# A higher planned cost for indirect DMAs in the list scheduler of a fused MoE, attention, MoE kernel

## The chip, the cores and the metric

The kernel runs on one core of a Trainium2 chip. A core has five engines with an instruction queue each: PE (TensorE, matmuls), DVE (VectorE), ACT (ScalarE), POOL (GpSimd) and SP (SyncE, which here only issues DMAs). Each engine takes its own queue in order, and the engines wait for each other by semaphores. The metric is the device time of one execution in microseconds (us). The kernel before was run nine times: median 531.88 us, lowest 528.12, highest 533.92.

## The reference

4,096 tokens (8 blocks of 512) with 128 features pass three layers, in f32:

```
x = x + 0.5 * ffn(layernorm(x))        # first expert layer,  key 0 in the kernel
x = x +  attention(layernorm(x))
x = x + 0.5 * ffn(layernorm(x))        # second expert layer, key 1

ffn(x):  n = layernorm(x) * gamma + beta
         probs = softmax(n @ router_w.T)            # 8 experts
         top_v, top_i = top_k(probs, 2);  gates = softmax(top_v)
         out = sum over e of comb[:, e] * ((silu(n @ g_e) * (n @ u_e)) @ down_e)    # d_ff 384
               + shared swiglu(n)                                                   # d_ff 128
attention(x): windows of 128 tokens; q, k, v; scores; the 32 largest scores of a row kept;
         softmax; times v; leaky relu; + x; layernorm
```

## The kernel before

**Stages.** The 8 blocks form two groups of 4 blocks (2,048 tokens); in names, `key` is the expert layer (0, 1) and `g` the group. For each (key, g) the kernel does this:

- `norm` normalizes a block, writes the rows to DRAM (`rows`), turns them on PE (`nTp`) and computes the logits (`lg`).
- `route` works out on DVE, with a few small matmuls (`rank`, `inv`), which token stands in which slot when the tokens are sorted by expert. It leaves `src` (the token of each slot) and `dst` (where a result goes).
- `experts` and `pair` do the expert work: 32 slot tiles of 128, and 39 pairs of a tile and an expert. A tile is fetched by an indirect DMA that POOL issues (`fetch`, L846: `xg<-rows,src`), four to a chunk. The chunk is turned on PE (`xTp`) and copied by ACT (`xT`). A pair is three matmuls for the gate (`pg`), three for the up projection (`pu`), a silu on ACT, a product on DVE (`s`), and three matmuls down (`y`), all 128x128x128 in f32. Four pairs share a `y` bank; ACT copies it (`yb`), and POOL issues one indirect DMA for each pair, which scatters the rows to DRAM (`put`, L962: `ys<-yb,dst`). Between two puts stands a 0.09 us memset.
- `shared` is the shared expert of a block (`pgs`, `pus`, `ysh`). `fetch_back` loads the scattered results (`yg`, SP or ACT queue), which waits for all 39 puts of the group; `combine` adds them on DVE (blocks 4 and 6 of the second layer on PE instead, `sum`, L1030).
- Between the two layers every block goes through `attention`, whose largest part is DVE's: four rounds of the 8 largest and their removal (`am8`, `tk`), each over four windows.

There are 128 fetches and 156 puts, 284 indirect DMAs in all.

**The order of the work.** No loop gives the order. Each step is recorded with `plan.op(engine, us, ...)`, where `us` is a planned duration, together with what it reads and writes, and gets a due time: the latest due time of what it needs plus a delay, or a floor set by the caller. `Plan.schedule` then plays the recorded steps: at each turn it takes the engine that can start earliest and, of the steps that can start there, the one due first. Every engine's queue is written out in the order found. The planned durations therefore decide the order, and nothing in the chip's run corrects it.

**The fillers.** `Plan.emit` does one more thing with the planned times. Where PE's planned idle time before a step is more than `IDLE` = 0.75 us, it puts matmuls into PE's queue that nobody reads (`unread`, L448), one for each `IDLE_US` = 0.22 us of the planned idle time less 0.4 us. They keep PE busy while it is planned to wait. They wait for nothing, and nobody waits for them but PE's queue. The profile counts two instructions for each.

```
idle = o.start - end
if idle > IDLE:
    us = IDLE_US * (COLD_FACTOR if o.start < COLD else 1.0)
    for _ in range(int((idle - IDLE_LEFT) / us)):
        self.idle()
```

**The constants.** `PACE` is the step of the due times from one fetch to the next for the four (key, g); `LAG`, `STRETCH` space the due times of the attention blocks; `ROUTE_STRETCH` and `ROUTE_B` those of the routing; `NORM_*` and `SHARED`, `SHARED1` those of the norms and the shared experts; `PAIRS`, `PUTS` parts of the routing; `FINISH` the last combination of the first group. A fetch is planned at 1.28 us of POOL (L846's `pool(1.28, ...)`), a put at 1.33 us.

Of the kernel before, what the change touches and what calls it, by code (L numbers as in the profile page):

```python
# [40 lines left out]
CH = 4  # L41
# [9 lines left out]
HANDOVER = {"PE": 0.25, "ACT": 0.2, "DVE": 0.2, "POOL": 0.25, "SP": 0.0}  # L51
OVERLAP = {"PE": 0.0, "ACT": 0.08, "DVE": 0.07, "POOL": 0.0, "SP": 0.0}
TABLE_LOAD = 1.28
COLD, COLD_FACTOR = 26.0, 1.8


# [2 lines left out]

PACE = (1.79, 2.74, 2.27, 0.89)
LAG, STRETCH, ROUTE_STRETCH = 9.73, -0.34, 3.22
NORM_B, NORM_LAG, NORM_STRETCH = 7.11, 1.83, 1.14
SHARED = ((28.42, 6.74), (33.75, 24.46))
SHARED1 = ((114.02, 8.44), (5.88, 23.46))
ROUTE_B = 38.08
PAIRS, PUTS = 0.5, 4.89
FINISH = 18.87


class Buf:
# [23 lines left out]
class Plan:  # L96
# [47 lines left out]
    def schedule(self):  # L144
# [38 lines left out]
        while len(order) < len(ops):  # L183
# [26 lines left out]
            if o.table and o.table != table:  # L210
                table = o.table
                o.start += TABLE_LOAD
            clock[o.eng] = o.start + us - OVERLAP[o.eng]
# [39 lines left out]
def kernel(  # L253
# [25 lines left out]
    plan = Plan(  # L279
        {  # L280
            "nT": 2 * GB,
            "h": GB, "a0": GB, "a1": GB, "a2": GB, "v": GB, "sc": GB,
            "ss": 2,
            **{t: 8 for t in ("st", "mv", "ve", "rstd", "nb", "am8", "nm", "rs")},
            "s": 4, "wt": WT, "xg": 4, "yb": 3, "yg": 4, "lanes": 4,
            **{t: 2 for t in ("lgs", "gates", "src", "off", "row", "to", "dst")},
            **{
# [12 lines left out]
    def pe(us, fn, r, w, **k):  # L300
        return plan.op("PE", us, fn, r, w, **k)

    def act(us, fn, r, w, **k):
        return plan.op("ACT", us, fn, r, w, **k)
# [4 lines left out]
    def pool(us, fn, r, w, **k):  # L309
        def run():  # L310
            last_put.clear()
            fn()

        return plan.op("POOL", us, run, r, w, **k)
# [4 lines left out]
    def buf(shape, tag, name, dtype=F32):  # L319
        return Buf(sb, shape, tag, name, dtype)  # L320

    def bank(kind, name):
        return Buf(ps, [P, W, P], "ps", name, kind=f"ps_{kind}")
# [208 lines left out]
    def norm(key, b, on_act=True):  # L532

        g, i = divmod(b, GB)
        r = routed[key, g]
        nm = f"_{key}_{b}"

        xb, xk = (lambda: xs[b]), [("x", b)]  # L540
        mv = stats(xb, xk, nm)
        rstd = scales(mv, nm, eps2)
        n = buf([P, W, H], "a0", f"n1_{key}_{b}")
        if on_act:
            normalize_act(n, xb, xk, rstd, shifts(mv, rstd, nm))
        else:
            normalize(n, xb, xk, mv, rstd)
        rows_t = r.rows[1 : 1 + GT, :].rearrange("(b p w) h -> b p w h", p=P, w=W)
        wr = load(0.6, lambda: rows_t[i], n, [n], [("rows", key, g, i)], lat=2.9)
        nT = r.nT[b] = buf([P, W, P], "nT", f"nT_{key}_{b}")  # L550
        tp = transposed(n, [n], f"nTp_{key}_{b}", hold=[nT])
        act(
            0.77,
            lambda: nc.scalar.activation(  # L554
                nT(), tp(), AF.Identity, bias=gb[:, 1:2], scale=gb[:, 0:1]
            ),
            [tp, "gb"], [nT],
        )
        lg = bank("m", f"lg_{key}_{b}")

        def logits():
            for w in range(W):
                nc.tensor.matmul(lg()[:, w, 0:NE], nT()[:, w, :], rwT, start=True, stop=True)  # L563

        pe(1.06, logits, [nT, "rwT"], [lg])
        dve(
            0.19,
            lambda: nc.vector.tensor_copy(r.lgs()[:, i * W : (i + 1) * W, :], lg()[:, :, 0:NE]),
            [lg], [(r.lgs, i)],
        )  # L570
        return wr

    def shared(key, b):

        nT = routed[key, b // GB].nT[b]
        pg, pu, ysh = (bank("m", f"{t}_{key}_{b}") for t in ("pgs", "pus", "ysh"))
        s, xk = buf([P, W, P], "ss", f"ss_{key}_{b}"), ("x", b)
        mm = nc.tensor.matmul
        up = pe(0.85, lambda: mm(pg(), gus[:, 0, :], nT(), start=True, stop=True),  # L579
                [nT, "gus"], [pg], hold=[s])  # L580
        act(0.6, lambda: nc.scalar.activation(s(), pg(), AF.Silu), [pg], [s], table="silu")
        pe(0.85, lambda: mm(pu(), gus[:, 1, :], nT(), start=True, stop=True),  # L582
           [nT, "gus"], [pu], after=[(up, 0.0)])
        dve(0.69, lambda: nc.vector.tensor_tensor(s(), pu(), s(), ALU.mult), [pu, s], [s])

        def down():
            for w in range(W):
                mm(ysh()[:, w, :], s()[:, w, :], dns, start=True, stop=True)  # L588

        pe(0.88, down, [s, "dns"], [ysh])  # L590
        dve(0.69, lambda: nc.vector.tensor_tensor(xs[b], ysh(), xs[b], ALU.add), [ysh, xk], [xk])
# [238 lines left out]
    before_ = [None] * 5  # L830

    def experts(key, g, pace):

        r, nm = routed[key, g], f"{key}_{g}"
        rows = [("rows", key, g, i) for i in range(-1, GB)]
        sizes = list(FIRST) if (key, g) == (0, 0) else []
        while sum(sizes) < NS:
            sizes.append(CH)
        fetched = []
        for c, n in enumerate(sizes):  # L840
            t0 = sum(sizes[:c])
            xg = buf([P, CH, H], "xg", f"xg_{nm}_{c}")
            for j in range(n):

                def fetch(t=t0 + j, j=j, xg=xg):
                    nc.gpsimd.indirect_dma_start(  # L846
                        xg()[:, j, :], None, r.rows,
                        bass.IndirectOffsetOnAxis(ap=r.src()[:, t : t + 1], axis=0),
                    )

                before_[2] = pool(1.28, fetch, [r.src, *rows], [(xg, j)], lat=3.6,
                                  after=[(before_[2], pace)])
                fetched.append(before_[2])
            tp = bank("m", f"xTp_{nm}_{c}")

            def turn(t0=t0, n=n, xg=xg, tp=tp):
                for w in range(n):
                    nc.tensor.transpose(tp()[:, w, :], xg()[:, w, :], ident)  # L858

            pe(0.11 * n, turn, [(xg, j) for j in range(n)], [tp])  # L860

            def fill(t0=t0, n=n, tp=tp):
                nc.scalar.activation(  # L863
                    xT[:, t0 * P : (t0 + n) * P].rearrange("p (w t) -> p w t", t=P),
                    tp()[:, 0:n, :], AF.Identity, bias=gb[:, 1:2], scale=gb[:, 0:1],
                )

            act(0.25 + 0.13 * n, fill, [tp, "gb"], [("xT", t0 + j) for j in range(n)])

            upto = NT if t0 + n == NS else t0 + n  # L870
            for t in range(t0, upto):
                first = t0 + (t - t0) // CH * CH
                pair(r, key, g, t, pace, fetched[min(t, NS - 1)], first, min(first + CH, upto))

    def pair(r, key, g, t, pace, came, first, upto):

        nm, group = f"{key}_{g}", f"ys_{key}_{g}"
        c, j = divmod(t, CH)
# [4 lines left out]
        y, yb = r.y, r.yb  # L883
# [73 lines left out]
        for i in range(a, b):  # L957
            def put(t=c * CH + i, i=i):
                if last_put:
                    nc.gpsimd.memset(apart, 0.0)  # L960
                last_put.append(t)
                ins = nc.gpsimd.indirect_dma_start(  # L962
                    r.ys, bass.IndirectOffsetOnAxis(ap=r.dst()[:, t : t + 1], axis=0),
                    yb()[:, i, :], None,
                ).ins

                tc.declare_no_dep(ins, group=group, reason="rows of other tokens")
                tc.add_to_no_dep_group(group, ins)

            plan.op("POOL", 1.33, put, [(yb, i), r.dst], [(group, c * CH + i)], lat=3.4)  # L970

    def fetch_back(key, b):

# [167 lines left out]
    def blocks(g):  # L1141
        return range(g * GB, (g + 1) * GB)
# [6 lines left out]
    rows = [norm(0, b, b % 2 == 1) for b in blocks(0)]  # L1149
    load_rest(rows)  # L1150
    def at(us, stretch=1.0):
        plan.floor, plan.stretch = us, stretch

    for g in range(NG):
# [4 lines left out]
        for i, b in enumerate(blocks(g)):  # L1159
            at(SHARED[g][0] + i * SHARED[g][1])  # L1160
            shared(0, b)
        at(ROUTE_B * g, 2.0 * g)
        route(0, g)
        at(0.0)
    for g in range(NG):
        experts(0, g, PACE[g])
    for g in range(NG):
# [14 lines left out]
        for i, b in enumerate(blocks(g)):  # L1182
            at(start + SHARED1[g][0] + SHARED1[g][1] * i)
            shared(1, b)
        at(0.0)
        experts(1, g, PACE[2 + g])
        diag = {b: weigh(b) for b in blocks(g) if b in LAST_ON_PE}
        for b in sorted(blocks(g), key=lambda b: b % 2):
            if g == 0:
                at(plan.ops[-1].due + FINISH, 2.0)  # L1190
            if b in diag:
# [42 lines left out]
```

## Time and profile before

| | |
|---|---|
| median of nine runs | 531.88 us |
| the profiled execution | 532.83 us, its span 531.0 us |
| PE busy | 501.5 us (94%), 31.8 us of it fillers |
| DVE, ACT, POOL busy | 376.5 us (71%), 276.0 us (52%), 369.2 us (70%) |
| granted PE clock | 0.992 of full speed |
| first expert pair starts | 49.30 us |
| first pair of (1,0) | 293.53 us |
| first pair of (1,1) | 426.47 us |
| last `y` ends, last `sum` begins | about 511.5 us, 520.4 us |

The span runs from the first to the last profiled instruction. A row of a group of instructions reads: line, engine, operation, what it writes <- what it reads, how often, then total busy time, mean nanoseconds of one, the engine's idle time just before them, and what ended most of that. A row of a timeline reads: start, duration, engine, line, operation, names, count, and in brackets the idle time of the engine before it and what ended it; rows of one engine may overlap a little, since an instruction can start before the one ahead has ended.

### The profile page before, as it was taken

How to read it: one execution, taken by the hardware profiler on the slowest of the kernel's cores; microseconds unless marked ns; L12 is line 12 of the kernel's file. 1: busy time of each engine (PE TensorE's matmuls, PEld its weight loads, DVE VectorE, ACT ScalarE, POOL GpSimd, SP SyncE). 2: the span in 40 equal slices, each digit the busy share in tenths (PEclk: the TensorE clock that was granted, in tenths of full speed). 3: DMA queues.
4: the chain of work that ended last, by engine and by line, in shares of the span. 5: the costliest groups of instructions: out<-in, count | busy, mean ns of one | idle time of the engine just before them, and what ended most of it. 6: DMA issues, size and time to landing. Idle time of an engine off the chain costs nothing.

```text
span 531.0 us, 13493 instructions
## 1 busy us (share of the span) xinstructions
PE 501.5 (94%) x4064; PEld 466.1 (88%) x4064; DVE 376.5 (71%) x1440; ACT 276.0 (52%) x588; POOL 369.2 (70%) x484
## 2 busy tenths in 40 slices
PE   3999999999979999899998999999999989999996
PEld 2878899999969899889987889989998889999996
DVE  6569944984418999995489799998478768445413
ACT  4822433333324799896630588897665224343310
POOL 7204787788876888878645788888845777878840
PEclk9999999999989999999999899999999999999999
DMA  7940211111359534537627545364775272211125
GB/s 231 329 159 22 56 50 46 51 49 51 95 158 339 185 106 136 187 105 226 206 66 233 156 124 153 102 204 137 215 221 153 76 232 84 74 51 51 52 86 188
DMA packets 39611, 72.27 MB, mean 136 GB/s; under 512 B 7604, under 2 KB 17848, under 8 KB 39544
## 3 DMA queue, kind: packets, MB, share of 16 engines
q1 hardware_dynamic: 29880, 51.73, 31.6%
q0 software_dynamic: 9088, 18.63, 11.5%
q10 hardware_dynamic: 576, 1.05, 0.5%
q8 instruction: 38, 0.62, 0.5%
q14 instruction: 29, 0.24, 0.2%
HBM read 54.86 MB, written 16.52 MB: 134 GB/s over the span
## 4 chain that ended last, share of the span: by engine, by line
PE 57%; DVE 23%; ACT 7%; POOL 4%; issue 4%; DMA 3%; DVEq 0%; POOLq 0%; ACTq 0%
PE pg L924 15%; PE y L940 14%; PE pu L924 14%; DVE tk L1088 5%; DVE am L1084 4%; DMA xg<-rows,src 3%; PE unread L448 3%; DVE s L935 2%; PE lg L563 2%; POOL ys L962 2%; PE pgs L579 2%; PE ysh L588 2%; POOL xg L846 2%; PE xTp L858 2%; PE pus L582 2%
## 5 line engine op out<-in xcount | busy, mean ns | idle before, releaser
L962 POOL DMA_INDIRECT ys<-yb,dst x156 | 160.4, 1028 | 60.1 <-ACT yb L954 29.4
L846 POOL DMA_INDIRECT xg<-rows,src x128 | 129.2, 1009 | 71.5 <-issue 31.8
L924 PE MATMUL pg<-xT,wt 128*128 (+1 forms) x936 | 134.3, 280 | 4.8 <-ACT xT L863 1.6
L924 PE MATMUL pu<-xT,wt 128*128 (+1 forms) x936 | 131.3, 277 | 0.0
L940 PE MATMUL y<-ew,s 128*128 x936 | 130.0, 276 | 1.0 <-DVE s L935 0.7
L924 PEld LDWEIGHTS pg<-xT,wt 128*128 128x128 f32 x936 | 119.0, 194 | 11.7 <-issue 4.3
L932 ACT ACTIVATE s<-pg 128x384 f32<-128x384 f32 x156 | 75.9, 491 | 99.9 <-PE pg L924 94.4
L940 PEld LDWEIGHTS y<-ew,s 128*128 128x128 f32 x936 | 117.1, 192 | 5.6 <-issue 3.2
L924 PEld LDWEIGHTS pu<-xT,wt 128*128 128x128 f32 x936 | 118.6, 194 | 1.0 <-issue 0.5
L935 DVE TENSOR_TENSOR s<-pu,s 128x384 f32<-128x384 f32 x156 | 85.1, 549 | 40.2 <-PE pu L924 29.6
L899 DVE COPY wt<-egu 128x768 f32 x78 | 44.8, 574 | 56.7 <-PE pu L924 55.9
L954 ACT COPY yb<-y 128x512 f32<-128x512 f32 (+1 forms) x60 | 26.1, 436 | 45.0 <-PE y L940 35.5
L999 DVE SCALAR_TENSOR_TENSOR x<-yg,gates,x 128x128 f32<-128x128 f32 x112 | 34.6, 372 | 10.6 <-DMA yg<-ys 10.6
L863 ACT ACTIVATE xT<-xTp,gb 128x512 f32<-128x512 f32 (+2 forms) x34 | 25.5, 756 | 26.7 <-PE xTp L858 26.7
L448 PEld LDWEIGHTS unread<-ident 128*128 128x128 f32 x264 | 31.0, 192 | 2.1 <-issue 2.1
L448 PE MATMUL unread<-ident 128*128 128x128 f32 x264 | 31.8, 275 | 0.0
L858 PE MATMUL xTp<-ident,xg 128*128 128x128 f32 x128 | 20.7, 276 | 6.3 <-DMA xg<-rows,src 6.3
L1088 DVE MATCH_REPLACE8 tk<-am,tk 128x128 f32<-128x128 f32 x96 | 25.3, 273 | 0.0
L499 ACT ACTIVATE n<-x,nb,rstd 128x128 f32<-128x128 f32 x56 | 22.8, 484 | 4.5 <-DVE nb L479 4.5
L563 PEld LDWEIGHTS lg<-rwT,nT 128*128 128x128 f32 x128 | 22.1, 261 | 3.3 <-ACT nT L554 2.2
L858 PEld LDWEIGHTS xTp<-ident,xg 128*128 128x128 f32 x128 | 15.2, 141 | 9.3 <-DMA xg<-rows,src 7.7
L563 PE MATMUL lg<-rwT,nT 128*128 128x8 f32 x128 | 21.7, 301 | 1.6 <-ACT nT L554 1.6
(177 smaller groups left out, 686.0 us busy)
## 6 DMA issues: line engine op xcount, KB each, us to landing
wt<-in_expert_gu SPq DMA_DIRECT2D x78, 384.0 KB, 3.5
yg<-ys SPq DMA_DIRECT2D x28, 256.0 KB, 4.2
rows<-n SPq DMA_DIRECT2D x16, 256.0 KB, 3.4
egu<-in_expert_gu SPq DMA_DIRECT2D x8, 384.0 KB, 6.5
ys<-yb,dst POOLq DMA_INDIRECT x156, 2.5
x<-in_x SPq DMA_DIRECT2D x8, 256.0 KB, 3.4
xg<-rows,src POOLq DMA_INDIRECT x128, 2.8
out_x<-x SPq DMA_DIRECT2D x8, 256.0 KB, 2.7
```

Of the source, the lines that this page charges most:

```text
L448: plan.idle = lambda: nc.tensor.matmul(unread, ident, ident, start=True, stop=True)
L563: nc.tensor.matmul(lg()[:, w, 0:NE], nT()[:, w, :], rwT, start=True, stop=True)
L846: nc.gpsimd.indirect_dma_start(xg()[:, j, :], None, r.rows, bass.IndirectOffsetOnAxis(ap=r.src()[:, t : t + 1], axis=0),)
L858: nc.tensor.transpose(tp()[:, w, :], xg()[:, w, :], ident)
L899: nc.vector.tensor_copy(to, egu[:, bass.ds(row, 2 * FF)])
L924: nc.tensor.matmul(p()[:, f, :], wt()[:, c * NF + f, :], xT[:, bass.ds(offs[1], P)], start=True, stop=True,)
L932: act(0.49, lambda: nc.scalar.activation(s(), pg()[:, 0:NF, :], AF.Silu), [pg], [s], table="silu")
L935: dve(0.56, lambda: nc.vector.tensor_tensor(s(), pu()[:, 0:NF, :], s(), ALU.mult), [pu, s], [s])
L940: nc.tensor.matmul(y()[:, j, :], s()[:, f, :], ew[:, bass.ds(offs[0] + f * H, H)], start=(f == 0), stop=(f == NF - 1),)
L962: ins = nc.gpsimd.indirect_dma_start(r.ys, bass.IndirectOffsetOnAxis(ap=r.dst()[:, t : t + 1], axis=0), yb()[:, i, :], None,).ins
L999: nc.vector.scalar_tensor_tensor(xs[b][:, w, :], yg[k]()[:, w, :], gates()[:, k, q : q + 1], xs[b][:, w, :], ALU.mult, ALU.add,)
L1088: ve.match_replace(tk()[:, w, :], m8()[:, w, :], src()[:, w, :], TAKEN)
```

## The change

The planned POOL time of each indirect DMA becomes one constant, 1.72 us, in place of 1.28 us (fetch) and 1.33 us (put). The planned time until the data has landed (3.6 and 3.4 us) stays. Paces, lags and floors get other values. No step is added to the computation or taken from it; the recorded steps and their operands are the same.

```diff
 TABLE_LOAD = 1.28
+INDIRECT = 1.72
 COLD, COLD_FACTOR = 26.0, 1.8
...
-PACE = (1.79, 2.74, 2.27, 0.89)
-LAG, STRETCH, ROUTE_STRETCH = 9.73, -0.34, 3.22
-NORM_B, NORM_LAG, NORM_STRETCH = 7.11, 1.83, 1.14
-SHARED = ((28.42, 6.74), (33.75, 24.46))
-SHARED1 = ((114.02, 8.44), (5.88, 23.46))
-ROUTE_B = 38.08
-PAIRS, PUTS = 0.5, 4.89
-FINISH = 18.87
+PACE = (1.79, 2.74, 1.81, 1.48)
+LAG, STRETCH, ROUTE_STRETCH = 10.16, -1.0, 9.06
+NORM_B, NORM_LAG, NORM_STRETCH = 7.11, 1.14, 1.08
+SHARED = ((25.08, 6.18), (33.75, 24.46))
+SHARED1 = ((143.03, 8.44), (5.88, 25.31))
+ROUTE_B = 18.79
+PAIRS, PUTS = -0.53, 5.28
+FINISH = 19.81
...
-                before_[2] = pool(1.28, fetch, [r.src, *rows], [(xg, j)], lat=3.6,
+                before_[2] = pool(INDIRECT, fetch, [r.src, *rows], [(xg, j)], lat=3.6,
                                   after=[(before_[2], pace)])
...
-            plan.op("POOL", 1.33, put, [(yb, i), r.dst], [(group, c * CH + i)], lat=3.4)
+            plan.op("POOL", INDIRECT, put, [(yb, i), r.dst], [(group, c * CH + i)], lat=3.4)
```

## The prediction

> **What bounds the kernel now.** I read the page first, then the windows by stage, then the timelines of POOL and PE. On the page PE carries the span: 94% busy. But 31.8 us of its 501.5 us are fillers, matmuls that nobody reads, 264 records or 132 fillers.
>
> ```profile
> span 531.0 us, 13493 instructions
> ...
> PE 501.5 (94%) x4064; PEld 466.1 (88%) x4064; DVE 376.5 (71%) x1440; ACT 276.0 (52%) x588; POOL 369.2 (70%) x484
> ...
> L448 PE MATMUL unread<-ident 128*128 128x128 f32 x264 | 31.8, 275 | 0.0
> ```
>
> The windows cut the span at the first pair, the first pair of (1,0), of (1,1), and the last `y`. A row gives the length, then each engine's busy time:
>
> ```profile
> 49.30:290.15 240.85, 233.01 (x1935) 216.96 (x1936) 179.31 (x675) 127.93 (x267) 181.42 (x224) 0.99 0.42 128
> 290.15:426.47 136.32, 131.87 (x1061) 120.50 (x1059) 112.51 (x478) 94.21 (x210) 103.50 (x123) 0.99 0.52 154
> 426.47:511.47 85.00, 82.60 (x730) 81.82 (x731) 47.18 (x107) 30.48 (x60) 66.06 (x97) 1.00 0.28 86
> ```
>
> Between the first pair and the last `y` PE idles 7.8 + 4.5 + 2.4 = 14.7 us of 462. Whatever is added to PE's queue there finds almost no gap to hide in. This is the reading on which the forecast rests.
>
> POOL's timeline shows what an indirect DMA costs when POOL has nothing to wait for:
>
> ```profile
> 154.56 0.96 POOL L846 DMA_INDIRECT xg<-rows,src  x1 [0.30 <-issue]
> 155.83 0.95 POOL L846 DMA_INDIRECT xg<-rows,src  x1 [0.30 <-issue]
> ...
> 494.33 0.99 POOL L962 DMA_INDIRECT ys<-yb,dst  x1 [0.23 <-issue]
> 495.32 0.09 POOL L960 MEMSET apart<- 1x1 f32 x1
> 495.63 0.96 POOL L962 DMA_INDIRECT ys<-yb,dst  x1 [0.21 <-issue]
> ```
>
> Start to start it is 1.27 us for a fetch and 1.30 us for a put. The old planned costs (1.28, 1.33) are right; 1.72 us is not what this trace shows. The scheduler will plan PE waits for POOL that do not come, and `emit` fills planned waits with matmuls that do.
>
> PE's timeline shows the price of a filler, and the one long wait in the middle:
>
> ```profile
> 146.13 0.49 PE L858 MATMUL xTp<-ident,xg 128*128 128x128 f32 x3
> 149.75 0.33 PE L858 MATMUL xTp<-ident,xg 128*128 128x128 f32 x1 [3.13 <-DMA xg<-rows,src]
> 149.95 1.16 PE L940 MATMUL y<-ew,s 128*128 x6
> 151.33 1.62 PE L924 MATMUL pg<-xT,wt 128*128 x6 [0.22 <-PE y L940]
> 152.75 1.37 PE L924 MATMUL pu<-xT,wt 128*128 x6
> ...
> 511.47 9.10 PE L448 MATMUL unread<-ident 128*128 128x128 f32 x80
> 520.41 0.39 PE L1030 MATMUL sum<-x,ident 128*128 128x128 f32 x2
> ```
>
> The 40 fillers at the end take 511.47 to 520.41, 8.94 us: 0.2235 us each, on PE alone. There they are free, since the results are only back at 520.73:
>
> ```profile
> 520.73 1.14 DVE L999 SCALAR_TENSOR_TENSOR x<-yg,gates,x 128x128 f32<-128x128 f32 x4 [10.39 <-DMA yg<-ys]
> ```
>
> **The change, part by part.** *Fillers.* In the built program's list of PE's instructions there are 132 fillers before and 492 after; all other PE work is the same in kind and number. By stage, before to after: ahead of the first pair 26 to 33; (0,0) up to the first chunk of (0,1) 1 to 48; from there to the first pair of (1,0) 50 to 140; to the first pair of (1,1) 15 to 117; to the end 40 to 154. 360 more at 0.2235 us are **+80.5 us** of PE work, which waits for nothing and cannot be skipped.
>
> *What they replace.* A filler is free where PE would have waited. The most it can replace is the 14.7 us of idle time and the slow matmuls after an idle stretch; the least is nothing. The waits for fetched rows are the ones that a PE slowed by fillers no longer meets: 3.13 us above, 0.51 + 0.85 at 216, 0.23 + 0.45 + 0.57 at 291, 0.79 at 282.7 (a product on DVE), 1.35 at 433.8; together 7.9. After the first and third of these the clock row falls (0.66 in 149.75 to 154.80, 0.55 in 293.50 to 297.30), and the next matmuls run 2.0 and 2.1 us longer than at the usual 0.67 us per three. I take both as gone: 7.9 + 4.1 = **-12.0 us**, with the ends 0 and 14.7 + 4.1 = 18.8. The rest of the idle time is short waits after register loads (0.2 to 0.7 us, "issue") that have no filler in front of them; they stay.
>
> The Trainium skill ("TensorE: Matmul & The Clock Gate", Part 1) speaks for fillers: after about 3.4 us of idle TensorE runs at half rate until it has been busy as long. By that an idle stretch costs about 1.7 us beside itself (estimate from the page), and 3.13 us or scattered gaps near 291 would not have cost it. The trace shows that they did. With the page's 1.7 us for one stretch the sum below is 2.4 us higher.
>
> *The tail.* 40 fillers become 114 ahead of `sum`: 25.5 us for 8.9. The real need is what the trace shows from the last `y` to the landing of `yg`, 9.2 us: two copies by ACT, the last put at 512.22, its landing, the loads issued at 514.46. POOL's list ends in the same puts, and POOL has no backlog there (it waits for `yb` before the last three). So 16.5 us of the tail are pure loss; they are in the 80.5.
>
> *POOL's order.* In (0,0) the list alternates four fetches and four puts, 8 x 1.3 = 10.4 us for a chunk (10.75 at the 1.344 us mean of 65.75 to 84.70); PE's chunk with 16 fillers is 8.5 + 3.6 = 12.1 us. POOL stays ahead. In (1,1) POOL issues 29 fetches in a row, 37 us, before the first put, and the fifth `y` bank needs a `yb` buffer that this put frees. From the first fetch (9 us before the first pair) PE has 20 gate and up pairs (26.8), 16 `y` (10.7) and seven turns (3.1): 49.6 us. The first four puts have landed after 37 + 5.2 + 2.5 = 44.7. No wait, and the 37 fillers in front of that bank (8.3 us) are lost too. Its cover if POOL were slow is these 8.3 + 4.9 us. DMAs on SP and POOL keep their number; seven more 0.09 us memsets on POOL have its slack (30% idle) as cover, else 7 x 0.3 = 2.1 us. ACT's table loads fall from 24 to 22 (2 x 1.28 us on an engine at 52%): nothing.
>
> *Head.* 18 fillers for 25 stand in front of `inv`, which in the trace starts at 43.90 with the fillers' end. That gives 1.6 us back, but 13 more and two shared-expert steps then stand before the first turned rows. Following PE's list at the trace's durations I get the first pair at 50.2 for 49.3: +0.9, where +1.6 is already counted with the seven added fillers: **-0.7 us**.
>
> *Attention of group 1.* Its top-k now stands closer together. From the first `am8` of block 4 to the last row sum of block 7 DVE's list has 16 rounds of 0.78 + 1.04 and 16.5 us of smaller steps, 45.6 us; PE's list has 41.8 us, fillers included, from block 4's scores to the turn of block 7. PE is late by **+4 us**. Bounds: 0, if the rest of DVE's order is kinder; 17, if DVE idles in both groups' attention stretches (45.6 and 51.8 us) as much as in 290 to 426 (17%). I take the one that follows from the list.
>
> *Sum* on the profiled execution: 531.0 + 80.5 - 12.0 - 0.7 + 4 = 602.8 us of span. That execution took 1.8 us more than its span (532.83) and 0.95 more than the median shown (531.88): **603.5 us**.
>
> **The rivals.**
> 1. *Fillers fit better than I think.* All 18.8 us vanish and attention costs nothing: 531.0 + 80.5 - 18.8 - 0.7 = 592.0, time 593. For: every filler stands where some wait was planned. Against: the "issue" gaps have none.
> 2. *Attention becomes the bound.* DVE waits for PE, which is behind its fillers, and PE then waits for DVE: +17 instead of +4, with only the 8 us of waits for rows gone: 531.0 + 80.5 - 8 - 0.7 + 17 = 619.8, time 621. For: DVE is 112.5 of 136.3 us busy in that stage now. Against: the fillers before those turns were put there for this wait.
> 3. *Not slower.* The fillers would have to run much faster than at the end of the trace, say hidden between other matmuls. Without them the sum is 531 - 8.7 = 522, so 360 of them may cost 10 us: under 0.03 us each against 0.2235 measured at the end and 0.23 at 38.3 (5.58 us for 25). POOL as the bound does not help: a PE queue that holds 552 us of matmuls at full rate cannot end at 531.
> 4. *The change does what it says because 1.72 us is POOL's real cost somewhere.* Then waits are real where fillers stand; but they would be in the trace of before as PE idle time, and only 14.7 us are. This is rival 1 at most.
>
> **How the numbers follow.** Forecast (597 to 609) 0.6; rival 1 (589 to 597) 0.14; rival 2 (609 to 625) 0.22; rivals 3 and 4 on the other side 0.02; the rest beyond 625. The range takes in both bounds: 592 to 621. Within 0.5% of before, about what can be told from no change: 0.01; faster 0.01; slower 0.98.
>
> **What would show it.** In the page after: the filler row with 984 records and about 110 to 119 us; PE busy near 580 us; POOL's share down to about 62%, the DMAs' means still 1.0 us. In PE's timeline: 114 fillers (228 records) of about 25 us before `sum`, with `yg` landed some 16 us before their end; runs of 12 fillers ahead of each turn in (0,0) with the fetched rows long landed; no 3 us wait for rows. Wrong would be: long PE waits in (0,0) or (1,1) with DMA as releaser (POOL slower than 1.3 us), waits over 10 us for `tk` in group 1 (rival 2), or the same useful matmuls at another pitch than 0.67 us per three.

## The result and the profile after

The changed kernel takes 616.18 us (median of 20 runs, 613.47 to 619.25) where the kernel before takes 531.14 us beside it: ratio 1.1603, 95% interval 1.1583 to 1.1623. The forecast was 603.5 us, range 592 to 621. The profiled execution took 616.34 us, its span is 614.6 us; the sum of the prediction gave a span of 602.8, so it is 11.8 us short. A ratio compares the means of the executions in the chip's faster state alone, so where the time shown for the kernel before also covers slower ones (645.83 us below), it is not the quotient of the two times shown.

The page after, the lines that answer to those of before:

```profile
span 614.6 us, 14994 instructions
...
PE 584.2 (95%) x4784; PEld 544.1 (89%) x4784; DVE 379.8 (62%) x1440; ACT 274.6 (45%) x586; POOL 370.4 (60%) x491
...
L963 POOL DMA_INDIRECT ys<-yb,dst x156 | 156.8, 1005 | 104.9 <-ACT yb L955 77.6
L847 POOL DMA_INDIRECT xg<-rows,src x128 | 130.0, 1015 | 63.6 <-issue 32.6
...
L449 PE MATMUL unread<-ident 128*128 128x128 f32 x984 | 117.4, 275 | 0.0
```

PE is busy 82.7 us longer (584.2 for 501.5), with 720 more records, all of them fillers. DVE, ACT and POOL do nearly what they did, in a longer span; an indirect DMA still takes 1.0 us of POOL, and POOL idles more than before.

The windows after, cut at the first pair, the first pair of (1,0), that of (1,1) and the last `y`. (The prediction's second cut, 290.15, lies 3.4 us ahead of the first pair of (1,0), at 293.53; its sum of idle time, 14.7 us, doesn't depend on that.) Columns: start and end, length, busy time of PE, PEld, DVE, ACT and POOL with records, granted clock, DMA share, GB/s:

```profile
50.20:331.80 281.60, 271.22 (x2233) 249.40 (x2231) 184.71 (x678) 129.50 (x267) 181.76 (x225) 1.00 0.36 111
331.80:487.51 155.71, 150.74 (x1244) 139.47 (x1245) 115.73 (x495) 92.41 (x208) 103.98 (x124) 1.00 0.48 148
487.51:578.00 90.49, 90.44 (x806) 90.06 (x807) 41.69 (x87) 29.14 (x58) 62.72 (x93) 1.00 0.17 51
```

PE idles 10.4 + 5.0 + 0.1 = 15.5 us in them; before it was 14.7. The time looks like matmuls, and the chain of work that ended last says the same: PE 75%, with the fillers alone at 13%. The experiments below show that this reading is not the whole of it.

POOL's timeline after, late in (1,1), and PE's and DVE's around the end:

```profile
576.85 0.96 POOL L963 DMA_INDIRECT ys<-yb,dst  x1 [0.21 <-issue]
577.80 0.09 POOL L961 MEMSET apart<- 1x1 f32 x1
578.12 0.96 POOL L963 DMA_INDIRECT ys<-yb,dst  x1 [0.23 <-issue]
```

```profile
576.89 1.82 PE L941 MATMUL y<-ew,s 128*128 x12
578.54 25.62 PE L449 MATMUL unread<-ident 128*128 128x128 f32 x228
604.00 0.39 PE L1031 MATMUL sum<-x,ident 128*128 128x128 f32 x2
```

```profile
590.50 1.14 DVE L1000 SCALAR_TENSOR_TENSOR x<-yg,gates,x 128x128 f32<-128x128 f32 x4 [12.79 <-DMA yg<-ys]
```

A put is still 1.27 us start to start, not 1.72. The 114 fillers ahead of `sum` take 25.5 us. The results have landed at 590.5, and `sum` could have started some 13.5 us before it does. These 13.5 us are pure loss, as forecast in kind.

In (0,0) PE's queue shows what the new order of a chunk looks like:

```profile
109.91 0.83 PE L941 MATMUL y<-ew,s 128*128 x6
110.58 0.39 PE L449 MATMUL unread<-ident 128*128 128x128 f32 x2
111.19 0.94 PE L941 MATMUL y<-ew,s 128*128 x6 [0.22 <-DVE s L936]
111.97 2.84 PE L449 MATMUL unread<-ident 128*128 128x128 f32 x24
114.65 0.60 PE L859 MATMUL xTp<-ident,xg 128*128 128x128 f32 x4
115.08 0.83 PE L449 MATMUL unread<-ident 128*128 128x128 f32 x6
116.11 0.94 PE L925 MATMUL pg<-xT,wt 128*128 x6 [0.20 <-ACT xT L864]
```

Twelve fillers stand ahead of the turn, as forecast. But one filler stands ahead of a product that is late and three between the turn and its own pairs, and even behind these PE waits 0.2 us for DVE and for ACT. So a product and a copy are late at this turn. Before shows such a wait for a product once in (0,0) (0.21 us at 111.18); after has both at three turns.

### The profile page after: what moved, and what is told of

The parts are those of the page before. It is cut to its first block, busy times and chain, and to the rows that moved or that the text cites. A ratio compares the mean times of both kernels' runs of the same rounds, so it can differ in the third digit from the quotient of the medians.

```text
span 614.6 us, 14994 instructions
## 1 busy us (share of the span) xinstructions
PE 584.2 (95%) x4784; PEld 544.1 (89%) x4784; DVE 379.8 (62%) x1440; ACT 274.6 (45%) x586; POOL 370.4 (60%) x491
## 4 chain that ended last, share of the span: by engine, by line
PE 75%; DVE 16%; ACT 5%; issue 1%; DMA 1%; POOL 1%; DVEq 0%; ACTq 0%
PE pg L925 16%; PE y L941 16%; PE pu L925 15%; PE unread L449 13%; DVE tk L1089 5%; DVE am L1085 3%; PE ysh L589 2%; PE pgs L580 2%; PE lg L564 2%; PE pus L583 2%; DVE s L936 1%; PE xTp L859 1%; ACT xT L864 1%; ACT n L500 1%; PE sum L1031 1%
## 5 line engine op out<-in xcount | busy, mean ns | idle before, releaser
L963 POOL DMA_INDIRECT ys<-yb,dst x156 | 156.8, 1005 | 104.9 <-ACT yb L955 77.6
L925 PE MATMUL pg<-xT,wt 128*128 (+1 forms) x936 | 132.1, 277 | 5.7 <-ACT xT L864 2.1
L925 PEld LDWEIGHTS pg<-xT,wt 128*128 128x128 f32 x936 | 117.4, 192 | 14.5 <-ACT xT L864 6.5
L941 PEld LDWEIGHTS y<-ew,s 128*128 128x128 f32 x936 | 115.7, 192 | 9.1 <-DVE s L936 5.6
L925 PEld LDWEIGHTS pu<-xT,wt 128*128 128x128 f32 x936 | 117.1, 192 | 0.5 <-issue 0.5
L449 PE MATMUL unread<-ident 128*128 128x128 f32 x984 | 117.4, 275 | 0.0
L449 PEld LDWEIGHTS unread<-ident 128*128 128x128 f32 x984 | 113.9, 192 | 2.1 <-issue 2.1
L1000 DVE SCALAR_TENSOR_TENSOR x<-yg,gates,x 128x128 f32<-128x128 f32 x112 | 31.6, 352 | 19.8 <-DMA yg<-ys 19.8
L473 POOL TENSOR_TENSOR rstd<-ve,mhalf 128x4 f32<-128x4 f32 x16 | 16.5, 1037 | 10.2 <-ACT ve L471 10.2
L513 PE MATMUL nTp<-ident,n 128*128 128x128 f32 x64 | 13.6, 356 | 9.0 <-DVE n L490 8.6
```

The costliest lines, as they stand in the source:

```text
L449: plan.idle = lambda: nc.tensor.matmul(unread, ident, ident, start=True, stop=True)
L925: nc.tensor.matmul(p()[:, f, :], wt()[:, c * NF + f, :], xT[:, bass.ds(offs[1], P)], start=True, stop=True,)
L941: nc.tensor.matmul(y()[:, j, :], s()[:, f, :], ew[:, bass.ds(offs[0] + f * H, H)], start=(f == 0), stop=(f == NF - 1),)
L963: ins = nc.gpsimd.indirect_dma_start(r.ys, bass.IndirectOffsetOnAxis(ap=r.dst()[:, t : t + 1], axis=0), yb()[:, i, :], None,).ins
L1000: nc.vector.scalar_tensor_tensor(xs[b][:, w, :], yg[k]()[:, w, :], gates()[:, k, q : q + 1], xs[b][:, w, :], ALU.mult, ALU.add,)
```

## The experiments

The theories:

- **A, the fillers.** The prediction's: the new order is about as good as the old one, and 360 more matmuls in PE's queue are the loss, since no wait comes where they stand. (In the expectations of the earlier runs, further down, A grants that some of the fillers cover real waits, and C says that the new order is as good as the old one.)
- **B, the order.** The order of the queues itself makes PE wait; the fillers stand in those waits and cost little of their own.

The two differ in what is left when the fillers are changed and the order is kept.

### Order and fillers exchanged

These two runs settle most of it, so they come first. The recorded steps of both kernels are the same, 2,417 in the same numbering. So the fillers of each kernel can be written down as a table (number of the step that they precede, how many) and put into the other kernel's queues. Here a run of the kernel before takes 530.88 us, as in the result.

The old order with the fillers of after (492):

```diff
+FILLERS = {
+    83: 13, 89: 2, 150: 18, 514: 1, 524: 12, 527: 3, 549: 1, 559: 12, 562: 3, 584: 1,
...
+    2061: 33, 2064: 3, 2208: 37, 2278: 3, 2399: 114,
+}
...
-                idle = o.start - end
-                if idle > IDLE:
-                    us = IDLE_US * (COLD_FACTOR if o.start < COLD else 1.0)
-                    for _ in range(int((idle - IDLE_LEFT) / us)):
-                        self.idle()
-                end = max(end, o.start + o.us + o.late)
+                for _ in range(FILLERS.get(o.n, 0)):
+                    self.idle()
```

> The queues of before, with the fillers of after: 492 in place of 132, each run in front of the step in front of which it stands in after (114 ahead of the first sum). Nothing else differs from before. Theory A (a filler is lost time in PE's queue, whatever the order): 360 more at 0.2235 us are 80.5 us less what this chip's longer waits cover, ratio 1.09 to 1.13. Theory B (the order of the queues is the loss, the fillers stand in its waits): the old order has few of these waits, but the fillers were not the cause, so 1.04 or less but for the 16.5 us of the tail. Both at work: 1.05 to 1.09.

Measured: 604.96 us, ratio 1.1381 [1.1332, 1.143], just above A's band.

The new order with the fillers of before (132), the same edit of `emit` in the changed kernel:

```diff
+FILLERS = {
+    150: 25, 345: 1, 364: 1, 1074: 4, 1297: 12, 1351: 2, 1363: 29, 1366: 3, 1503: 3, 1791: 2,
+    2055: 3, 2061: 4, 2064: 3, 2399: 40,
+}
```

> The queues of after, with the fillers of before: 132 in place of 492, each run in front of the step in front of which it stands in before (40 ahead of the first sum). Theory A (fillers are all): within 3% of before, ratio 1.03 or less. Theory B (order is all): 1.13 to 1.16, as the changed kernel. By the kernels with 418, 346 and no fillers (13.5, 25 and 37.7 us less than the changed kernel) I expect some 34 us less than 739, ratio 1.09 to 1.11: the new order alone then costs about as much as the fillers do beyond what its waits cover.

Measured: 593.1 us, ratio 1.117 [1.1132, 1.1207], between the bands of A and B and a little above my own.

| time, ratio to before | fillers of before (132) | fillers of after (492) |
|---|---|---|
| order of before | 530.9 us, 1 | 604.96 us, 1.1381 |
| order of after | 593.1 us, 1.117 | 616.18 us, 1.1603 |

Both theories hold, and they overlap. The fillers alone cost 74 us, the order alone 62 us, and both together 85: some 51 us of the one stand in the other. Theory A nearly holds in the old order: 80.5 us of matmuls, 71.9 us more span (602.9 for 531.0). It is wrong for the kernel that was made: with the 132 old fillers in place of its 492 the changed kernel gets back 23 us, not 80.

The new order with the old fillers has the same 4,064 records of PE as before, but its page (span 589.6 us) shows them busy longer:

```profile
PE 522.2 (89%) x4064; PEld 478.4 (81%) x4064; DVE 380.2 (64%) x1440; ACT 274.3 (47%) x586; POOL 369.9 (63%) x491
```

Of the 58.6 us by which the span is above that of before, 37.9 are PE's idle time (67.4 for 29.5) and 20.7 are longer busy time (522.2 for 501.5), at a mean granted clock of 0.960 for 0.992. So the order's cost is waits and, behind them, slower matmuls.

PE's waits in that run show what the order does. Columns: engine, line and tile that wait, what for, us in total, times, longest:

```profile
PE y L942 <- DVE s L937: 13.6, 10, 4.0
...
PE xTp L860 <- DMA xg<-rows,src: 8.0, 5, 2.4
PE pg L926 <- ACT xT L865: 7.5, 8, 1.0
PE pTp L514 <- DVE sc L1105: 6.4, 2, 4.9
PE ysh L590 <- DVE held L807: 2.9, 1, 2.9
PE pTp L514 <- ACT xT L865: 2.9, 2, 2.6
```

Only the second line is what the planner fears, rows that POOL fetched late, and it is 8.0 us, where before has 6.3. The others are PE's dependences on DVE and ACT: a product `s` behind its pair, the copy `xT` behind a turn, scores (`sc`) behind their top-k, a routing step (`held`). PE's timeline of the same run in (0,0):

```profile
121.36 0.83 PE L926 MATMUL pu<-xT,wt 128*128 x6
122.03 0.83 PE L942 MATMUL y<-ew,s 128*128 x6
123.31 0.94 PE L942 MATMUL y<-ew,s 128*128 x6 [0.45 <-DVE s L937]
124.08 0.60 PE L860 MATMUL xTp<-ident,xg 128*128 128x128 f32 x4
125.64 0.94 PE L926 MATMUL pg<-xT,wt 128*128 x6 [0.96 <-ACT xT L865]
```

A chunk's turn stands directly ahead of its own pairs, and between the last up projection of a chunk (121.36) and its `y` (123.31) there is one other `y`; nothing else is left in PE's queue to lie in between. 0.45 + 0.96 us follow, at three chunks of (0,0). Some of the fillers of after are in those very places (the rows of 110.58 and 115.08 above).

The largest piece is the attention of group 1. The window from the turn of block 4's scores to that of block 7's, in the order before, old order with new fillers, new order with old fillers, and after:

```profile
318.40:359.40 41.00, 40.50 (x323) 36.79 (x323) 40.77 (x205) 37.30 (x81) 34.45 (x37) 1.00 0.49 149
```

```profile
347.90:401.20 53.30, 53.30 (x446) 50.35 (x445) 40.49 (x206) 38.03 (x81) 33.13 (x37) 1.00 0.38 113
```

```profile
357.00:390.50 33.50, 19.87 (x115) 18.00 (x116) 32.80 (x174) 22.95 (x52) 21.44 (x20) 0.72 0.23 68
```

```profile
362.60:395.00 32.40, 28.93 (x238) 26.97 (x239) 32.33 (x174) 23.21 (x52) 21.06 (x21) 1.00 0.21 61
```

After the start and end and the length come PE, PEld and DVE, so DVE's number is the third with a count in brackets. In the old order with its own fillers and in both runs of the new order DVE is busy with hardly a gap (40.77 of 41.00, 32.80 of 33.50, 32.33 of 32.40 us); only the old order with the added fillers leaves DVE waiting for PE. In the new order DVE is the bound of this stretch; in the old one PE is full as well (40.50 of 41.00). What differs is what PE is given to do beside the top-k. In PE's list the old order has 11 expert pairs there, 38.7 us of matmuls; the new one has 2 pairs, 12.0 us. The pairs that are missing come later (30 for 21 from there to the first pair of (1,1)), after the top-k. So in the new order with old fillers PE gives 33.5 us to 12.0 us of useful matmuls (13.6 us idle; mean granted clock 0.72) and does the other work later. After's 65 fillers there (14.5 us) are free: 33.5 us without, 32.4 with them. PE's timeline without and with:

```profile
362.39 0.66 PE L860 MATMUL xTp<-ident,xg 128*128 128x128 f32 x4
365.65 1.11 PE L514 MATMUL pTp<-ident,sc 128*128 128x128 f32 x4 [2.60 <-ACT xT L865]
366.56 1.48 PE L450 MATMUL unread<-ident 128*128 128x128 f32 x6
...
375.04 0.83 PE L514 MATMUL pTp<-ident,sc 128*128 128x128 f32 x4 [4.95 <-DVE sc L1105]
...
383.52 1.62 PE L942 MATMUL y<-ew,s 128*128 x6 [4.04 <-DVE s L937]
```

```profile
374.33 5.52 PE L449 MATMUL unread<-ident 128*128 128x128 f32 x48
380.25 0.63 PE L513 MATMUL pTp<-ident,sc 128*128 128x128 f32 x4 [0.39 <-DVE sc L1104]
...
383.06 4.63 PE L449 MATMUL unread<-ident 128*128 128x128 f32 x40
388.73 0.91 PE L941 MATMUL y<-ew,s 128*128 x6 [1.03 <-DVE s L936]
```

By stage: the useful matmuls of every step, at their pitch from the profile of before (0.67 us for three of 128x128x128 and so on), sum to 442.0 us in all four kernels. The table gives what each stage takes beyond them; in brackets the fillers in it, at 0.2235 us each.

| us beyond useful matmuls, up to | before | old order, new fillers | new order, old fillers | after |
|---|---|---|---|---|
| first pair | 31.0 (5.8) | 32.0 (6.9) | 35.0 (5.8) | 32.8 (7.4) |
| first turn of (0,1) | 2.7 (0.2) | 12.5 (11.2) | 8.0 (0.2) | 16.2 (10.7) |
| first turn of the attention of group 0 | 5.4 (0) | 7.0 (6.9) | 10.5 (0) | 13.1 (9.2) |
| first turned block of layer 1 (so the attention of group 0) | 2.3 (0) | 8.4 (6.9) | 10.9 (0) | 10.4 (4.7) |
| first pair of (1,0) | 17.7 (11.2) | 28.1 (17.4) | 24.8 (11.1) | 23.8 (17.4) |
| block 4's scores turned | 4.1 (0.4) | 4.6 (2.9) | 5.8 (0.4) | 4.4 (2.9) |
| block 7's scores turned | 2.2 (0.7) | 14.6 (14.5) | 21.5 (0.7) | 20.4 (14.5) |
| first pair of (1,1) | 6.1 (2.2) | 12.4 (8.7) | 12.4 (2.2) | 11.3 (8.7) |
| first `sum` | 12.4 (8.9) | 36.1 (34.4) | 11.3 (8.9) | 35.1 (34.4) |
| end | 5.3 | 5.3 | 7.3 | 5.3 |
| all | 89.0 (29.5) | 160.8 (110.0) | 147.6 (29.5) | 172.6 (110.0) |

From the third column to the fourth, 80.5 us of fillers are added and the time grows by 25.0 us. That loss stands in two places: ahead of `sum` and in (1,1) (+23.8) and in (0,0) (+8.2). Everywhere else the stages hardly move (+2.6 at most, mostly a little down): the fillers stand in waits that the order makes, and keep the clock up. From the first column to the third the order costs 58.6 us, 19.3 of it beside the top-k of group 1, and not one us of it in (1,1).

### Before these: fillers taken out, and the parts of the change

The other ten runs were made earlier, on three other chips, where the kernel before takes 640 to 646 us; each ratio is to runs of before on the same chip. The chips differ (more on that at the end), so these runs are read for differences only.

Without fillers, the changed kernel and the one before (the unread matmuls are left out, nothing else):

```diff
                 if idle > IDLE:
                     us = IDLE_US * (COLD_FACTOR if o.start < COLD else 1.0)
-                    for _ in range(int((idle - IDLE_LEFT) / us)):
-                        self.idle()
+                    pass
```

> The changed order with all 492 fillers left out. Theory A (the loss is matmul time that the fillers add to PE's queue, in places where no wait comes): 110 us of fillers go; of them some 60 us covered real waits (11.8 at the end, where the results landed 11.8 us after the last y; about 9 ahead of the first pair of (1,0), 7 ahead of that of (1,1), 13 in the attention of group 1, 9 in that of group 0, the rest in small pieces), so 616 - 50 = 566 us, between 550 and 585. Theory B (the new order of the queues is itself the loss, and the fillers only stand in its waits): 605 us or more. Theory C (the order is as good as the old one and fillers are all of it): 526 to 536 us.

> The order of before with all 132 fillers left out. Theory A: nearly all of its 29.5 us of fillers stand in waits that come (9.2 of 8.9 us at the end, a route chain at 277 to 292), 1.9 us ahead of inv do not, and a cold PE costs up to 2 us after each of three or four long gaps: 526 to 536 us, no change within 1%. Theory B says nothing else here. If fillers always cost their time, 502 us.

Measured: after without fillers 702.35 us, 1.0951 [1.0839, 1.1063]; before without fillers 648.84 us, 1.0103 [0.9996, 1.0211], against 645.83. C is refuted: without any filler the new order takes 53.5 us more than the old one, the first sign that the order itself costs. 1.0951 lies in the upper part of A's band (550 to 585 us are 1.04 to 1.10 of 531) and below B's. The old fillers are worth some 0 to 2%, not more than these runs can tell.

Only the last run of fillers cut to 40:

```diff
-                    for _ in range(int((idle - IDLE_LEFT) / us)):
+                    for _ in range(min(int((idle - IDLE_LEFT) / us), 40 if o.start > 500 else 1000)):
```

> The changed kernel with the last run of fillers cut from 114 to 40, nothing else. Theory A: sum can then start when the results have landed, 11.8 us after the last y and not 25.5 us: -13.7 us, 602.5 us (the full -16.5 if the landing is as quick as before). Theory B: no change, 616 us.

Measured: 725.11 us, 1.1299 [1.1186, 1.1413], by the ratio as A has it (602.5 us are 1.134 of 531).

The queues of after, but the fillers counted from start times that are played again in the fixed order with 1.3 us for an indirect DMA (346 fillers):

```diff
+REAL = 1.3
...
+    def replay(self, order):
...
+            for p, d in o.preds.items():
+                if p.us == INDIRECT and d == p.us + 0.03:
+                    d = REAL + 0.03
...
+            real = REAL if o.us == INDIRECT else o.us
...
         order, us = self.schedule()
+        self.replay(order)
```

> The changed order, every queue the same, but the fillers are counted from planned times that are played once more in that order with 1.3 us for an indirect DMA: 346 fillers for 492. Theory A: 146 x 0.2235 = 32.6 us fewer, and few new waits: 584 us, 580 to 592. Theory B: 610 us or more, since the waits come anyway.

Measured: 714.72 us, 1.1138 [1.1049, 1.1227], by the ratio in A's band (580 to 592 us are 1.09 to 1.115 of 531).

The planned cost alone (1.72 us, old paces and floors), and the three variants of after once more, on another chip:

```diff
+INDIRECT = 1.72
...
-                before_[2] = pool(1.28, fetch, [r.src, *rows], [(xg, j)], lat=3.6,
+                before_[2] = pool(INDIRECT, fetch, [r.src, *rows], [(xg, j)], lat=3.6,
...
-            plan.op("POOL", 1.33, put, [(yb, i), r.dst], [(group, c * CH + i)], lat=3.4)
+            plan.op("POOL", INDIRECT, put, [(yb, i), r.dst], [(group, c * CH + i)], lat=3.4)
```

> Before with the planned 1.72 us alone, old paces and floors. Its list has 501 fillers, 369 more than before. Theory A: +82.5 us of matmuls less what they replace, as in the changed kernel (there +80.5 gave +83.6 of span): 608 to 622 us where before takes 531, a ratio of 1.145 to 1.17. Rival (the paces and floors make the loss): ratio under 1.05.

> The changed order with all fillers left out, on another chip than the first time if there is one where before takes about 531 us. Theory A: ratio to before 1.03 to 1.10 (550 to 585 us). Theory B (the order alone is the loss): 1.14 or more. Theory C (the order is as good as the old one): 0.99 to 1.01.

> The changed kernel with the last run of fillers cut from 114 to 40. Theory A: -13.7 us against the changed kernel's 616.2, so 602.5 us, ratio 1.134. Theory B: ratio 1.16.

> The changed order with the fillers counted for 1.3 us indirect DMAs, 346 for 492. Theory A: 580 to 592 us, ratio 1.09 to 1.115. Theory B: ratio 1.15 or more.

Measured, against 644.16: the cost alone 759.62 us, 1.1817 [1.174, 1.1894]; after without fillers 701.1 us, 1.0891 [1.0816, 1.0965]; with the tail at 40, 725.46 us, 1.1242 [1.1149, 1.1334]; refilled 713.39 us, 1.1096 [1.1025, 1.1167]. The cost alone is above A's band (1.145 to 1.17); the other three repeat the first results, and without fillers the ratio is inside A's band (1.03 to 1.10), below B's 1.14.

The changed kernel itself there, and the paces and floors alone (planned costs of before):

```diff
-PACE = (1.79, 2.74, 2.27, 0.89)
...
-FINISH = 18.87
+PACE = (1.79, 2.74, 1.81, 1.48)
...
+FINISH = 19.81
```

> The changed kernel itself beside before on the chip of this call, as the anchor for the other runs: 616 us and a ratio of 1.16 where before takes 531. On the chip of the earlier calls, where before takes 645, theory A (fillers cost their time wherever no wait comes) gives the run with the last fillers cut, 725 us, plus 13.7: 739 us, a ratio of 1.145; theory B (fillers only stand in waits) gives the 702 us of the run without fillers, a ratio of 1.09.

> Before with the new paces and floors alone, the planned 1.28 and 1.33 us kept. Its list has 265 fillers, 133 more than before. Theory A: at most +29.7 us of fillers less what they replace: ratio 1.02 to 1.06. Rival (the paces and floors make the loss): ratio over 1.10.

Measured, against 640.42: the changed kernel 738.78 us, 1.1516 [1.1453, 1.158], A's 739 us; the paces alone 700.96 us, 1.0931 [1.0864, 1.0998].

What follows:

- The cost alone is the worst of the three (1.18), the paces alone cost 9% with only 265 fillers, and both together are better than the cost alone (1.15). So the new paces do soften the new cost, and each part by itself makes the kernel slower; these two runs don't separate order from fillers. My band for the paces alone was 1.02 to 1.06, and the rival's began at 1.10: neither.
- By number of fillers, the changed queues took 738.8 us with 492, 725 with 418, 714 with 346 and 702 with none. (The 346 are counted anew, not taken from the 418: 63 of them stand in the tail.) The first 74, those of the tail, cost some 13.5 us, nearly their full 16.5; the last 346 only some 12 us for 77 us of matmuls. In all, 492 fillers cost 37 us of 110; the first expectation had 50. So A's bands were met here, and yet the order costs by itself: A as these expectations put it leaves room for that.
- PE's timeline there without fillers has the same waits in group 1 as the run of the new order with old fillers:

```profile
435.06 1.06 PE L512 MATMUL pTp<-ident,sc 128*128 128x128 f32 x4 [2.60 <-ACT xT L863]
...
444.17 1.09 PE L512 MATMUL pTp<-ident,sc 128*128 128x128 f32 x4 [4.95 <-DVE sc L1103]
...
452.65 1.62 PE L940 MATMUL y<-ew,s 128*128 x6 [3.78 <-DVE s L935]
```

No kernel here is faster than the one before.

## Why the prediction was right and where it was wrong

The direction, the size of the filler term and the range were right. The likeliest case was not: its own band ended at 609, and 616 lies in the band of rival 2. The terms, in us of span:

| term of the sum | forecast | measured |
|---|---|---|
| 360 more fillers | +80.5 | +80.5 at 0.2235 us (114 of them took 25.46) |
| what they replace | -12.0 | -7.9 (the stages that got shorter beyond their fillers); -8.6 in the old order (71.9 left of 80.5) |
| head | -0.7 | +0.2 beyond the fillers there; first pair at 50.4, forecast 50.2 |
| attention of group 1 | +4 | +4.4 beyond the fillers there (5.9 for 1.5) |
| (0,0), attention of group 0 | 0 | +3.0 and +3.4 beyond the fillers |
| sum | +71.8 | +83.6 |

- **"What they replace"** was mis-sized. The waits for fetched rows did vanish: the list of PE's waits after has none with DMA as releaser. But the sum took 12.0 us for these and for matmuls at a slow clock, and the measurements give 7.9, or 8.6 by the exchange in the old order.
- **The step that failed** is the bound of the same term: "The most it can replace is the 14.7 us of idle time and the slow matmuls". That is the idle time of the old order. The new order makes 58.6 us of waits and slower matmuls of its own, and the added fillers take the place of 55.5 us of them (80.5 less the 25.0 that they cost there). Rival 4 has the same fault: "they would be in the trace of before as PE idle time". A trace shows the waits of the order that it ran, and of no other.
- **Why the sum came out near all the same.** With both changes made, PE's queue is full, so its length is the sum of what stands in it, whichever part one calls the cause. Counted with the fillers first, they are +71.9 (in the old order) and the new order on top of them +11.7; counted the other way, the order is +58.6 and the fillers on top of it +25.0. Both ways end at +83.6 us; only the exchange shows that 25.0 is what removing the fillers would give back. The forecast's whole +71.8 is what the fillers cost in the old order alone, and its order, +3.3 (0.7 down, 4 up), is too small even in that way of counting. That the range still took in the result is partly luck: the order's cost was left out, and so was nearly all of what the fillers cover of it.
- **"The scheduler will plan PE waits for POOL that do not come"** holds as far as it goes: POOL keeps its 1.27 us, and of the waits of the new order 8.0 us are for fetched rows. But other waits stand in the same places: the new list leaves PE nothing to put between a turn and its pairs, and little beside the top-k. That the planner does this because it holds the pairs back for POOL is how I read it; no run separates it from the new paces. I did not see these waits, though "Its top-k now stands closer together" was in the prediction.
- **Attention of group 1**: the +4 came out at +4.4 for a reason that I did not give, so the size is luck. PE is not late behind its fillers; DVE is the bound of that stretch, and the 65 fillers there are free. Rival 2 had half of the mechanism, PE waiting for DVE; its other half, DVE waiting for PE, did not come (DVE is busy 32.33 of 32.40 us), and that the time lies in its band does not confirm it.
- **The tail** was right: 25.5 us, of which the results needed 11.8 after the last `y` where I had 9.2, so 13.5 us of loss at the end where I had 16.5. The 37 fillers in (1,1) are lost as forecast: up to `sum`, after takes 23.8 us more than the new order with old fillers, against 24.8 for 74 and 37 fillers. The last stage is 2.0 us shorter (5.3 for 7.3), so 21.8 us are lost in all: the 13.5 and 8.3 for the 37.
- **POOL's order** was right: no long wait of PE with DMA as releaser in (0,0) or (1,1). **The (0,0) stage** was forecast as nothing beyond its fillers, and has +3.0, much of it from the late product and copy at three turns, shown above: 0.2 us of idle time each, but 0.4 us more than the matmuls' pitch from start to start (110.58 to 111.19, 115.08 to 116.11).
- **The clock.** The prediction took 4.1 us off for two cold stretches and set the page's figure beside it. After, the three windows shown have the clock at 1.00, so the cold stretches are gone; the exchange doesn't separate their 4.1 us from the rest. The other side was not in the prediction: the new order by itself lets the clock fall oftener (0.960 for 0.992).

Why the three other chips take a fifth more time for every kernel, and whether the parts of the change (cost alone, paces alone) stand in the same proportion on this chip, stays open: these two were run only there.

## What to carry to other kernels

Changed planned durations and paces do two things at once here: they reorder the work of every engine, and, where planned idle time is filled, they fill. To price such a change, price the new order by itself, from each engine's new list: look for stretches where one engine is full and count what the others are still given to do beside it. Idle time in the old trace bounds what can be saved in the old order, not what a new order will wait.

When a profile shows one engine 95% busy and part of that is work that nobody reads, its busy time says nothing about the cause. Take the filler out, or exchange order and filler, before calling either the loss.

## What the runs showed of the hardware

- TensorE's clock fell after 2.60 us of idle time. In the new order with old fillers PE runs at full rate up to 363.05 us, idles 2.60 us, and the next six records of fillers take 1.48 us where six take 0.83 otherwise (the rows at 362.39 to 366.56 above, and at 115.08 of after). The Trainium skill ("TensorE: Matmul & The Clock Gate", Part 1) puts that point at about 3.4 us of idle time; here 2.60 was enough. The granted clock over that stretch is 0.72, and 1.00 where fillers stand (the windows above).
- Keeping the clock up is worth little where another engine is the bound: the stretch of the top-k takes 33.5 us at 0.72 and 32.4 us at 1.00. Elsewhere its worth was not measured by itself.
- On three other chips the same programs take about a fifth longer: 640 to 646 us for the kernel before against 531, 738.8 for the changed one against 616.2, at a granted clock of 0.93 to 0.96. The trace of the changed kernel there has 65.5 us in which DVE's weight copies (`wt`) and 48.0 us in which ACT's silu (`s`) wait for releases that it can't place, which the trace here has not. The ratio after to before hardly differs (1.1516 against 1.1603). The cause was not found.
